# Moving one VectorE sum ahead of a scaled addition and a transposition in a graph layer and attention kernel

## The chip, the cores and the metric

The kernel runs on one core of a Trainium2 chip. The metric is device time in microseconds (us), the median of several executions. The engines are TensorE (PE in the profile, with its weight loads as PEld), VectorE (DVE), ScalarE (ACT), GpSimd (POOL) and SyncE (SP). In this kernel SP issues all DMAs of the main loop. Each engine works through its own list of instructions in order and waits on semaphores for the others.

## The reference

There are 64 batch elements of 256 nodes with 512 features, and one 256 x 256 graph. Two layers follow each other:

```python
# layer 0: graph layer, then residual and layer norm
mi, mj = x @ Wi.T, x @ Wj.T
a   = adj.astype(float);  deg = a.sum(axis=1)
out = deg[:, None] * (mi + b) + a @ mj
h   = layernorm(x + out)
# layer 1: attention over 8 heads of 64, masked by adj, then residual and layer norm
q, k, v = heads(h @ Wq.T + bq), heads(h @ Wk.T + bk), heads(h @ Wv.T + bv)
attn = softmax(where(adj == 0, -inf, q @ k.T / 8))
y    = layernorm(h + merge(attn @ v) @ Wo.T + bo)
```

All is float32. The change lies in layer 0, in the part that makes `mj`, and in the sum `x + deg * mi`.

## The kernel before

**Groups.** The elements are handled in 32 groups of two. A pass of the main loop (`for g in range(NG - 1)`, 31 passes, fully unrolled) does the attention of group g and, between its products, layer 0 of group g + 1. `b1` and `b2` are the first and the second element of a group. A row tile is 128 of the 256 nodes; `t` is 0 or 1.

**Products.** The dense products of layer 0 are done by blocks with seven products in place of eight. `l0_steps(b)` gives the steps of one element as a list of functions: `step1` to `step7` (each with one product of four matmuls on PE and what is done with its result), `neighbours` (the product with the graph), `take(1)` and `take(0)` (the residual sum and the statistics of the norm), and `give` and `send_h` for each row tile (the norm applied, and h sent to DRAM to be read back in another layout).

The steps around the change, in the names of the code:

- `step4` keeps `u2` (L542, DVE), `step5` copies a product into `mj[:, 1]` (L547, DVE).
- `step6` makes `u3` (L551, DVE). POOL adds it to `mj[:, 1]` (L552). `split(1)` then makes the high half `hi` on ACT (L524) and the low half `lo` = `mj` - `hi` on POOL (L525), since the graph product takes its operands in a shorter format and two halves keep the precision. At the end of the step `add_scaled(1, u3)` (L520, DVE) adds `deg * u3` to row tile 1 of `xh`, where the residual is gathered.
- `step7` makes `mj[:, 0]` from its product and `u2` (L561, DVE), and `split(0)` makes its two halves.
- `neighbours` multiplies `hi` and `lo` of both row tiles by the graph into `pa`, row tile 1 of `mj` first.
- `take(t)` adds `pa` to `xh` (L575, DVE) and computes the statistics (L453 to L459 on DVE, the power `rstd` on POOL, L461).

**Where they run.** `layer0(g)` cuts the steps of both elements into portions, and the main loop runs one portion after each pair of attention products. In the portion concerned stands also `turn_h(b1)`: a DVE transposition (L485) of the first element's h, which has come back from DRAM in the tile `hB`, into `hT`. The next portion starts after the last two value products of the pass and is written out by hand: first product of the output projection (`o[0]`), `neighbours`, `take(1)`, `take(0)`, first product of the query projection (`q[0]`), and so on. `multiply` (L844, POOL) scales the attention output, `divide` has the reciprocal of the denominators (L882, DVE) and the DMAs `spread` (L890), eight for each reciprocal. The first product of the output projection is added on POOL (L746, L747).

**What sets the order.** A scheduler orders the instructions of each engine by the order of the program and by times that it reckons for them. An instruction that goes through `in_order` keeps its place among the others of its engine that do; one that doesn't (`anywhere`) may be moved. All matmuls, the transpositions, and the operations of `take` and `give` are held in order; L561 and the scaled addition are not:

```python
def in_order(ins):
    tc.keep_in_program_order(ins)

def anywhere(ins):
    pass
```

The weight factors of layer 1 come from DRAM through a ring of 9 buffers (L442), the products of layer 0 and of the projections share three PSUM banks (tag "mm"), and `hi`, `lo`, `mj`, `hB` and `hT` have one buffer each. L740 (DVE) adds later products of the output projection to `xh` and frees their banks.

Of the kernel before, what the change touches and what calls it, by code (L numbers as in the profile page):

```python
# [12 lines left out]
ALU = mybir.AluOpType  # L13
# [211 lines left out]
def unshifted_path(ctx, tc, flag, x, adj, wiT, wjT, b0, wqT, bq, wkT, bk, wvT, bv, woT, bo, out):  # L225
# [16 lines left out]
    nc = tc.nc  # L242
# [26 lines left out]
    def bank(name):  # L269
        return ps_m.tile([P, 512], F32, tag="mm", name=name)  # L270

    def score_banks(name):
        return ps_s.tile([P, 2, 512], F32, tag="sc", name=name)
# [8 lines left out]
    def in_order(ins):  # L282

        tc.keep_in_program_order(ins)
# [4 lines left out]
    def matmul(*args, **kw):  # L289
        in_order(nc.tensor.matmul(*args, **kw))  # L290
# [5 lines left out]
    xh = {}  # L296
# [47 lines left out]
    deg = small.tile([P, NT], F32, tag="deg", name="deg")  # L344
# [51 lines left out]
    def blocks_of(w):  # L396
        return (w.rearrange("(h c p) (j o) -> p h c j o", h=2, p=P, j=2) if w is woT else
                w.rearrange("(p h c) (j o) -> p h c j o", h=2, p=P, j=2))

    sources = {}  # L400
    for name, w in (("wq", wqT), ("wk", wkT), ("wv", wvT), ("wo", woT)):
        src = blocks_of(w)
# [48 lines left out]
    def norm_stats(t, order=anywhere):  # L451
        st = small.tile([P, 6], F32, tag="st", name="st")
        order(nc.vector.bn_stats(st, t))  # L453
        mv = small.tile([P, 2], F32, tag="mv", name="mv")
        nc.vector.bn_aggr(mv, st)
        ve = small.tile([P, 1], F32, tag="ve", name="ve")
        nc.vector.tensor_scalar(ve, mv[:, 1:2], EPS, None, ALU.add)
        below = small.tile([P, 1], F32, tag="below", name="below")
        order(nc.vector.tensor_scalar(below, mv[:, 0:1], -1.0, None, ALU.mult))  # L459
        rstd = small.tile([P, 1], F32, tag="rstd", name="rstd")  # L460
        nc.gpsimd.tensor_tensor(rstd, ve, mhalf, ALU.pow)  # L461
        return below, rstd

    def norm_apply(t, below, rstd, order=anywhere):
        shift = small.tile([P, 1], F32, tag="shift", name="shift")
        order(nc.scalar.activation(shift, below, AF.Identity, scale=rstd))  # L466
        order(nc.scalar.activation(t, t, AF.Identity, bias=shift, scale=rstd))  # L467
# [31 lines left out]
            for step in left_steps(xS[b], in_order):  # L499
                step()  # L500

    def l0_steps(b):
        banks, k = {}, {}

        def product(name, left, n, first):
            if first:
                banks[name] = bank("po")
            for c in range(2):
                matmul(banks[name], left[:, c, :], w0[:, n, c, :], start=(first and c == 0),
                                 stop=(c == 1), skip_group_check=True)  # L510

        def raw(t, h):
            return xT[b][:, 2 * h:2 * h + 2, t * P:(t + 1) * P]

        def keeper(name):
            k[name] = p3.tile([P, D], F32, tag="lu", name=name)
            return k[name]

        def add_scaled(t, src):
            nc.vector.scalar_tensor_tensor(xh[b][:, t, :], src, deg[:, t:t + 1], xh[b][:, t, :],  # L520
                                           ALU.mult, ALU.add)

        def split(t):
            nc.scalar.copy(k["hi"][:, t, :], k["mj"][:, t, :])  # L524
            nc.gpsimd.tensor_tensor(k["lo"][:, t, :], k["mj"][:, t, :], k["hi"][:, t, :].bitcast(F32),  # L525
                                    ALU.subtract)

        def step1():
            product("x", raw(0, 0), B11, True)
            nc.scalar.copy(keeper("u1"), banks["x"])  # L530

        def step2():
            product("w", raw(1, 1), T4, True)
            add_scaled(1, banks["w"])

        def step3():
            product("x", raw(0, 1), B21, False)
            add_scaled(0, banks["x"])

        def step4():  # L540
            product("y", xS[b]["S2"], T2, True)
            nc.vector.tensor_add(keeper("u2"), banks["y"], k["u1"])  # L542

        def step5():
            product("z", xS[b]["S1"], T1, True)
            k["mj"] = p1.tile([P, NT, D], F32, tag="mj", name="mj")
            nc.vector.tensor_copy(k["mj"][:, 1, :], banks["z"])  # L547

        def step6():
            product("y", xS[b]["S3"], T3, False)  # L550
            nc.vector.tensor_add(keeper("u3"), banks["y"], k["u1"])  # L551
            nc.gpsimd.tensor_tensor(k["mj"][:, 1, :], k["mj"][:, 1, :], k["u3"], ALU.add)  # L552

            k["hi"] = p1.tile([P, NT, D], F32R, tag="hi", name="hi")
            k["lo"] = p1.tile([P, NT, D], F32R, tag="lo", name="lo")
            split(1)
            add_scaled(1, k["u3"])

        def step7():
            product("z", xS[b]["S4"], B22, False)  # L560
            nc.vector.tensor_add(k["mj"][:, 0, :], banks["z"], k["u2"])  # L561
            split(0)

        stats = {}

        def neighbours():
            k["pa"] = score_banks("pa")
            for i in (1, 0):
                for n, (j, part) in enumerate((j, part) for j in (1, 0) for part in ("hi", "lo")):
                    matmul(k["pa"][:, i, :], graph[:, j, i * P:(i + 1) * P], k[part][:, j, :],  # L570
                           start=(n == 0), stop=(n == 2 * NT - 1))

        def take(t):
            r = xh[b][:, t, :]
            in_order(nc.vector.tensor_add(r, k["pa"][:, t, :], r))  # L575
            stats[t] = norm_stats(r, in_order)

        def give(t):
            norm_apply(xh[b][:, t, :], *stats[t], in_order)


        return [step1, step2, step3, step4, step5, step6, step7, neighbours, lambda: take(1), lambda: take(0),
                lambda: give(1), lambda: send_h(b, 1), lambda: give(0), lambda: send_h(b, 0)]

# [10 lines left out]
    def send_h(b, t):  # L595
        i = b % NB
        if t == 1:
            h_cols[b] = dram.tile([D // P, N, P], F32, tag=f"h{i}", name="h_cols")
        nc.sync.dma_start(out=h_cols[b][:, t * P:(t + 1) * P, :].rearrange("q p n -> p q n"),
                          in_=xh[b][:, t, :].rearrange("p (q n) -> p q n", n=P))  # L600
        if t == 0:
            hB[b] = p1.tile([P, N // R, P], F32, tag="hB", name="hB")
            nc.sync.dma_start(out=hB[b].rearrange("p a n -> p (a n)"),
                              in_=h_cols[b].rearrange("q (r a) n -> (q r) (a n)", r=R))
# [63 lines left out]
    def second_late(steps):  # L668
        return [steps[0], steps[2], steps[1], *steps[3:]]
# [30 lines left out]
    def qk_steps(g, store, tag, bias, diff, early=False):  # L700

        def new_store():
            store[g] = p1.tile([P, NC, NB * N], F32, tag=tag, name=tag)

        def place(i, j):
            return store[g][:, 2 * j:2 * j + 2, i * N:(i + 1) * N]

        def biased(b):
            def evict(dst, ps):
                for m in range(2):  # L710
                    nc.scalar.activation(dst[:, m, :], ps[:, m, :], AF.Identity, bias=b[:, m:m + 1], scale=1.0)
            return evict

        def last(dst, ps, addend):
            for m in range(2):
                nc.vector.scalar_tensor_tensor(dst[:, m, :], ps[:, m, :], diff[:, m:m + 1],
                                               addend[:, m, :], ALU.add, ALU.add)

        return qkv_steps(g, True, new_store, place, biased(bias), biased(diff), last, early)
# [175 lines left out]
    def layer0(g):  # L895

        b1, b2 = NB * g, NB * g + 1

        def item(f, *args):
            return lambda: f(*args)  # L900

        p, q = l0_steps(b1), l0_steps(b2)
        return [p[:3] + [item(turn_x, b2)] + p[3:4],
                p[4:7] + [item(sum_x, b2), item(add_bias, b2)] + q[:1],
                p[7:10], p[10:] + q[1:3],
                q[3:6] + [item(turn_h, b1)] + q[6:7],
                q[7:], [item(turn_h, b2)]]

    def run(steps):
# [6 lines left out]
    def order_of(name):  # L916
        return [(name, n) for n in RIGHT]

    for g in range(-1, NG - 1):
        o, q, k, v = (order_of(name) for name in ("wo", "wq", "wk", "wv"))  # L920
# [18 lines left out]
    p, q = l0_steps(0), l0_steps(1)  # L939
# [19 lines left out]
    k = second_late(qk_steps(0, kT, "kT", bk_sb, bkd, True))  # L959
# [22 lines left out]
    for g in range(NG - 1):  # L982
# [20 lines left out]
        q = second_late(qk_steps(g + 1, qT, "qT", bq_sb, bqd))  # L1003
        k = second_late(qk_steps(g + 1, kT, "kT", bk_sb, bkd, True))
# [7 lines left out]
        k = with_output_bias(g + 1, k)[2:]  # L1012
# [101 lines left out]
```

## Time and profile before

| | |
|---|---|
| runs | 3117.25 us median of 3 (3113.67 to 3117.7) |
| profiled execution: span and the time listed for it | 3114.5 us |
| TensorE clock granted | 0.999 |
| PE, PEld busy | 3066.7 us (98%), 2125.4 us (68%) |
| DVE busy | 2200.1 us (71%) |
| POOL busy | 1505.3 us (48%) |
| ACT busy | 967.4 us (31%) |
| DMA engines busy | 48.4% in the main queue |

"Busy" is the time in which an engine executed instructions; its waits and the issue of DMAs are not in it. In the lines of a timeline the columns are the start, the duration (both us), the engine, the line of the code, the operation, what it writes and reads (`out<-in`), the shapes, how many were merged into the line, and in brackets the idle time before it with what ended it. In the list of waits a line names who waited for whom, with the total, how often, and the longest. All matmuls are recorded by one helper (L290), so that they are told apart by the tiles they write.

### The profile page before, as it was taken

To read this page: it belongs to the slowest core of one execution; us is meant where nothing else is said; L and a number is where in the kernel's file an instruction comes from. 1 tells how busy PE (TensorE), PEld (TensorE's weight loads), DVE (VectorE), ACT (ScalarE), POOL (GpSimd) and SP (SyncE) were. 2 spreads that over 40 slices of the span, in tenths; PEclk is the share of its full clock that TensorE was granted. 3 is DMA by queue.
4 is the path that set the end of the run, shared out by engine and by line. 5 is a ranking of instruction groups with operands and counts; after the bars stand their busy time and mean duration, and the time that the engine had idled before them with its cause. 6 is when DMAs were issued, how large, how long until landed. Compare 5 with 4: busy or idle time off the path is not lost. (4 is left out here: it accounts for less than half of the span.)

```text
span 3114.5 us, 42683 instructions
## 1 busy us (share of the span) xinstructions
PE 3066.7 (98%) x14598; PEld 2125.4 (68%) x14598; DVE 2200.1 (71%) x3298; ACT 967.4 (31%) x1861; POOL 1505.3 (48%) x1255
## 2 busy tenths in 40 slices
PE   8999999999999999999999999999999999999998
PEld 4667766677766777666776667776677766677665
DVE  6776677766777767777667776677766777767775
ACT  2322333323333323332233332333332333323332
POOL 2544445544545445454454554454543545445453
PEclk9999999999999999999999999999999999999999
DMA  7355544455444555345553445544455444555333
GB/s 253 116 151 156 166 122 131 133 155 165 143 123 125 157 165 152 117 129 151 156 166 119 129 135 158 164 142 124 124 159 164 144 123 125 158 158 158 119 106 103
DMA packets 410395, 447.28 MB, mean 144 GB/s; under 512 B 40896, under 2 KB 300224, under 8 KB 409792
## 3 DMA queue, kind: packets, MB, share of 16 engines
q1 hardware_dynamic: 410176, 444.50, 48.4%
q8 instruction: 120, 1.97, 0.3%
q14 instruction: 99, 0.81, 0.1%
HBM read 340.79 MB, written 70.25 MB: 132 GB/s over the span
## 5 line engine op out<-in xcount | busy, mean ns | idle before, releaser
L461 POOL TENSOR_TENSOR rstd<-ve,mhalf 128x1 f32<-128x1 f32 x256 | 140.4, 552 | 715.8 <-DVE below L459 715.8
L812 POOL TENSOR_TENSOR pk<-pe 128x512 f32<-128x512 f32 x256 | 322.5, 1276 | 327.6 <-ACT pe L809 327.5
L290 PE MATMUL po<-w,xS 128*128 128x512 f32 x1024 | 462.4, 599 | 0.4 <-DVE xS L478 0.4
L290 PE MATMUL st<-hS,factor 128*128 128x256 f32 x2048 | 453.5, 380 | 5.1 <-DVE xh L740 3.8
L290 PEld LDWEIGHTS st<-hS,factor 128*128 128x128 f32 x2048 | 388.9, 190 | 60.1 <-DVE xh L740 6.4
L809 ACT ACTIVATE pe<-pe 128x1024 f32<-128x1024 f32 x256 | 270.9, 1058 | 379.0 <-DVE pe L805 379.0
L290 PE MATMUL po<-w,xT 128*128 128x512 f32 x768 | 354.5, 605 | 13.1 <-DVE xT L485 11.1
L290 PE MATMUL st<-hT,factor 128*128 128x256 f32 x1536 | 352.6, 380 | 0.7 <-ACT hT L622 0.7
L290 PEld LDWEIGHTS po<-w,xS 128*128 128x128 f32 x1024 | 190.1, 191 | 235.9 <-issue 206.4
L805 DVE TENSOR_TENSOR pe<-ps,maskT 128x1024 f32<-128x1024 f32 x256 | 298.1, 1195 | 35.3 <-PE ps L290 35.3
L290 PEld LDWEIGHTS st<-hT,factor 128*128 128x128 f32 x1536 | 292.2, 190 | 41.7 <-ACT hT L622 0.9
L882 DVE RECIPROCAL rden<-den 128x256 f32<-128x256 f32 x127 | 223.1, 1757 | 92.2 <-PE den L290 89.0
L290 PEld LDWEIGHTS po<-w,xT 128*128 128x128 f32 x768 | 144.7, 192 | 181.2 <-issue 163.3
L290 PE MATMUL ps<-qT,kT 64*128 64x256 f32 x2048 | 265.0, 393 | 0.0
L290 PE MATMUL pav<-pe,v_sb 128*64 128x256 f32 x2048 | 250.2, 386 | 1.9 <-ACT pe L809 1.8
L883 POOL TENSOR_TENSOR rtot<-rtot,rden 128x256 f32<-128x256 f32 x127 | 92.3, 727 | 329.7 <-DVE rden L882 329.7
L740 DVE TENSOR_TENSOR xh<-st,xh 128x512 f32<-128x512 f32 x186 | 144.6, 777 | 136.4 <-PE st L290 136.4
L290 PEld LDWEIGHTS pav<-pe,v_sb 128*64 128x64 f32 x2048 | 135.3, 136 | 154.0 <-issue 95.4
L290 PEld LDWEIGHTS ps<-qT,kT 64*128 64x128 f32 x2048 | 184.7, 187 | 77.8 <-issue 51.3
L290 PE MATMUL st<-factor,hS 128*128 128x256 f32 x1024 | 234.8, 383 | 0.0
L525 POOL TENSOR_TENSOR lo<-mj,hi 128x512 fp32r<-128x512 f32 x128 | 175.2, 1378 | 107.3 <-ACT hi L524 107.3
L290 PE MATMUL st<-factor,oS 128*128 128x256 f32 x992 | 224.3, 380 | 0.0
(115 smaller groups left out, 4679.5 us busy)
## 6 DMA issues: line engine op xcount, KB each, us to landing
xB<-in_x_dram SPq DMA_DIRECT2D x256, 128.0 KB, 3.8
xh<-in_x_dram SPq DMA_DIRECT2D x64, 512.0 KB, 4.2
factor<-wq SPq DMA_DIRECT2D x128, 256.0 KB, 4.3
factor<-wk SPq DMA_DIRECT2D x128, 256.0 KB, 3.0
factor<-wv SPq DMA_DIRECT2D x128, 256.0 KB, 2.7
spread<-rden SPq DMA_DIRECT2D x1016, 32.0 KB, 1.9
factor<-wo SPq DMA_DIRECT2D x124, 256.0 KB, 3.2
h_cols<-xh SPq DMA_DIRECT2D x124, 256.0 KB, 2.4
```

Source lines behind the costliest of these rows:

```text
L290: in_order(nc.tensor.matmul(*args, **kw))
L461: nc.gpsimd.tensor_tensor(rstd, ve, mhalf, ALU.pow)
L525: nc.gpsimd.tensor_tensor(k["lo"][:, t, :], k["mj"][:, t, :], k["hi"][:, t, :].bitcast(F32), ALU.subtract)
L740: nc.vector.tensor_add(dst, src, dst)
L805: nc.vector.tensor_add(pe.rearrange("p j t q -> p j (t q)"), ps.rearrange("p j t q -> p j (t q)"), maskT.rearrange("p t q -> p (t q)").uns ...
L809: in_order(nc.scalar.activation(flat, flat, AF.Exp, scale=QSCALE, accum_out=etot[:, NB * g + i, pr:pr + 1]))
L812: nc.gpsimd.tensor_tensor(pk, pe[:, :, 0, :], pe[:, :, 1, :], ALU.add)
L882: nc.vector.reciprocal(rden, den)
L883: nc.gpsimd.tensor_tensor(rtot, rtot, rden, ALU.add)
```

## The change

`l0_steps` gets an argument `late`, which only the second element's steps in the main loop set. With it, `add_scaled(1, u3)` is left out of `step6` and issued in `take(1)`, in order, right before `pa` is added to the same rows; the sum of `step7` is held in order; and `layer0` runs `step7` whole before the transposition of the first element's h rather than after it.

```diff
-    def l0_steps(b):
+    def l0_steps(b, late=False):
         banks, k = {}, {}
+        order = in_order if late else anywhere
...
         def add_scaled(t, src):
-            nc.vector.scalar_tensor_tensor(xh[b][:, t, :], src, deg[:, t:t + 1], xh[b][:, t, :],
-                                           ALU.mult, ALU.add)
+            return nc.vector.scalar_tensor_tensor(xh[b][:, t, :], src, deg[:, t:t + 1], xh[b][:, t, :],
+                                                  ALU.mult, ALU.add)
...
             split(1)
-            add_scaled(1, k["u3"])
+            if not late:
+                add_scaled(1, k["u3"])
 
         def step7():
             product("z", xS[b]["S4"], B22, False)
-            nc.vector.tensor_add(k["mj"][:, 0, :], banks["z"], k["u2"])
+            order(nc.vector.tensor_add(k["mj"][:, 0, :], banks["z"], k["u2"]))
             split(0)
...
         def take(t):
             r = xh[b][:, t, :]
+            if late and t == 1:
+                in_order(add_scaled(1, k["u3"]))
             in_order(nc.vector.tensor_add(r, k["pa"][:, t, :], r))
...
-        p, q = l0_steps(b1), l0_steps(b2)
+        p, q = l0_steps(b1), l0_steps(b2, True)
...
-                q[3:6] + [item(turn_h, b1)] + q[6:7],
+                q[3:7] + [item(turn_h, b1)],
```

## The prediction

> **What bounds the kernel.** I read the page first (busy shares), then the list of waits for PE alone, then the timeline of one loop pass engine by engine. The page:
>
> ```profile
> PE 3066.7 (98%) x14598; PEld 2125.4 (68%) x14598; DVE 2200.1 (71%) x3298; ACT 967.4 (31%) x1861; POOL 1505.3 (48%) x1255
> ```
>
> PE is occupied from end to end; no other engine comes near. So only what shortens or removes a PE wait can pay, and only what creates one can cost. The list of waits, PE's own (columns: total us, times, longest):
>
> ```profile
> PE pa L290 <- POOL lo L525: 15.9, 31, 0.5
> PE po L290 <- DVE xT L485: 11.1, 2, 8.3
> PE st L290 <- DVE xh L740: 3.8, 5, 1.2
> ```
>
> The first wait happens 31 times, once per pass of the main loop: the neighbour product `pa` waits for the low half `lo`, which POOL makes. The second lies in the prologue, out of the change's reach. The third is rare; I return to it. Now the pass that starts its first-element transposition at 1000.78 us. Timeline of DVE (start us, duration us):
>
> ```profile
> 999.00 1.86 DVE L520 SCALAR_TENSOR_TENSOR xh<-u,deg,xh 128x512 f32<-128x512 f32 x1
> 1000.78 2.14 DVE L485 STREAM_TRANSPOSE hT<-hB 128x1024 f32<-128x1024 f32 x1
> 1002.83 0.64 DVE L561 TENSOR_TENSOR mj<-po,u 128x512 f32<-128x512 f32 x1
> 1003.40 1.74 DVE L882 RECIPROCAL rden<-den 128x256 f32<-128x256 f32 x1
> 1006.99 0.69 DVE L575 TENSOR_TENSOR xh<-pa,xh 128x512 f32<-128x512 f32 x1 [1.86 <-PE pa L290]
> ```
>
> The sum of row tile 0 (L561) has no idle time before it: it is not waiting for its product but standing behind 1.86 us of scaled addition and 2.14 us of transposition. POOL in the same pass, after its L552 of 999.04 to 1000.31 (the sum of row tile 1):
>
> ```profile
> 1001.04 1.29 POOL L525 TENSOR_TENSOR lo<-mj,hi 128x512 fp32r<-128x512 f32 x1 [0.73 <-ACT hi L524]
> 1004.20 1.29 POOL L525 TENSOR_TENSOR lo<-mj,hi 128x512 fp32r<-128x512 f32 x1 [1.86 <-ACT hi L524]
> 1005.44 1.29 POOL L844 TENSOR_TENSOR aoT<-aoT,spread 128x512 f32<-128x512 f32 x1
> 1006.68 0.73 POOL L883 TENSOR_TENSOR rtot<-rtot,rden 128x256 f32<-128x256 f32 x1
> 1007.37 1.27 POOL L746 TENSOR_TENSOR xh<-xh,u 128x512 f32<-128x512 f32 x1
> 1008.60 2.36 POOL L747 TENSOR_TENSOR xh<-xh,u 128x1024 f32<-128x1024 f32 x1
> 1010.91 1.06 POOL L461 TENSOR_TENSOR rstd<-ve,mhalf 128x1 f32<-128x1 f32 x2
> ```
>
> The second L525 (row tile 0) idles 1.86 us, then runs to 1005.49, and PE continues at once:
>
> ```profile
> 1003.97 0.58 PE L290 MATMUL pa<-hi,graph 128*128 128x512 f32 x1
> ...
> 1004.62 0.39 PE L290 MATMUL pa<-hi,graph 128*128 128x512 f32 x1
> 1005.54 0.50 PE L290 MATMUL pa<-lo,graph 128*128 128x512 f32 x1 [0.52 <-POOL lo L525]
> ...
> 1006.79 0.38 PE L290 MATMUL st<-hT,factor 128*128 128x256 f32 x1
> ```
>
> The same eight matmuls in the prologue, where nothing is late:
>
> ```profile
> 53.74 0.58 PE L290 MATMUL pa<-hi,graph 128*128 128x512 f32 x1
> ...
> 55.80 1.02 PE L290 MATMUL st<-hT,factor 128*128 128x256 f32 x4
> ```
>
> **What the Trainium skill says.** "Perfetto Trace Analysis", section "Identifying the Most-Contended Engine", warns that matmul busy time is no measure of headroom, because matmuls are pipelined. The trace agrees: the wait is booked as 0.52 us, but the group takes 1006.79 - 1003.97 = 2.82 us against 55.80 - 53.74 = 2.06. I therefore price the stall by start times, not by idle time. "SBUF — State Buffer", section "Who interferes with whom", says that a VectorE instruction with two SBUF inputs and a GpSimd instruction that reads SBUF exclude each other, the second to start waiting in full, while one SBUF input does not contend. The trace agrees: the scaled addition from `u3` (two SBUF inputs) took 1.86 us beside L552, ending 0.55 after L552 let go at 1000.31, while the same operation with a PSUM input takes 0.74 (mean of that group), beside POOL or not.
>
> **The change, part by part.** In each of 31 passes it leaves every instruction and every DMA as it was; three DVE instructions change places. No DMA moves in the program's order, but the transfers that wait for these results shift with them.
>
> (a) *The sum goes ahead of addition and transposition.* It needs its product. Products of this element arrive 1.72 us apart (L547 at 996.55 and L551 at 998.27 both waited for PE), so this one arrives at 998.27 + 1.72 = 999.99. DVE is free since L551 ended at 998.96. The sum runs 999.99 to 1000.68, with one SBUF input, so L552 beside it doesn't matter. Being held in order now, it makes the transposition behind it wait for PE as well; that is the new wait. The transposition then runs 1000.68 to 1002.82, 0.1 us earlier than before: the wait costs nothing because the addition used to stand in its place.
>
> (b) *What follows the sum.* ACT finishes the high half of row tile 1 at 1000.96, then does that of tile 0 to about 1001.6. POOL does L525 of tile 1 to 1002.33 as before and of tile 0 to 1003.62. PE wants it 0.23 us after 1004.62, at 1004.85. Slack 1.2 us: the stall is gone. Worth 2.82 - 2.06 = 0.76 us per pass; 31 x 0.76 = **23.6 us**.
>
> (c) *The reciprocal* follows the transposition at 1002.82 instead of 1003.40 and ends at 1004.56. The eight `spread` DMAs that wait for it on SP start 0.6 us earlier, and so does what SP has behind them (weight factors, the sends of h).
>
> (d) *The scaled addition* now stands before L575. I take it behind the reciprocal, at 1004.56. POOL has moved up: L844 runs 1003.62 to 1004.91 (its last `spread` was issued by 999.75 and such DMAs land in 1.9 us by the page). So the addition waits for the port until 1004.91 and ends 0.55 later, at 1005.46. Bounds: 0.74 us unblocked, 1.86 us as seen, so 1005.3 to 1006.4. L575 can start only when `pa` is complete, 1006.99 - 0.76 = 1006.23. DVE idled 1.86 us there; that idle time is the cover. If it were gone, L575, the statistics, the powers on POOL and the sends of h would be late; even the upper bound makes L575 only 0.2 us late.
>
> (e) *Does something late eat the gain?* The statistics' powers (L461) wait on POOL behind L883, L746 and L747. From 1005.46 these take 0.73 + 1.27 + 2.36, so L461 starts at 1009.82 instead of 1010.91: 1.09 us earlier, while PE gains only 0.76. The chain from there (shift and scaling on ACT, two sends to DRAM, the load of hB, the second element's transposition, its sums, then L740 freeing a bank for PE) keeps its durations, so it gains 0.33 us on PE. That shortens the third wait of PE, 5 x 0.33 = 1.7 us of its 3.8.
>
> Sum: -23.6 - 1.7 = -25.3 us. The profiled execution's span is 3114.5 us and that is the time listed for it; the median of the runs lies 2.75 us above. The saving is in the loop, so it applies to both: 3117.25 - 25.3 = **3092 us** (span about 3089).
>
> **Rivals.** (1) *Given back at the second element's h.* DVE waits for hB at only 6 transpositions, and PE for the following L740 at only 5 passes, yet the margin is small. If the chain of (e) doesn't move, for instance because transfers take longer when issued closer together, PE gains 0.76 and then loses what exceeds the margin; in the pass above the wait was already 0.4. A give-back of 0.3 to 0.5 us per pass leaves 31 x 0.26 to 0.46 = 8 to 14 us: 3103 to 3109. Against it: POOL's earlier powers.
>
> (2) *The addition is put ahead of the reciprocal*, since only the addition is held in order. It would start at 1002.82, be blocked by L525 to 1003.62, end at 1004.17; the reciprocal ends at 1005.91, 0.8 us later than before, and so do the `spread` DMAs. L461 starts at about 1010.3, 0.6 us earlier, against 0.76 on PE: 5 waits grow by 0.16, about 1 us. L844's second product slips too; PE uses it over 2 us later (1013.22 to 1015.42). 3117 - 23.6 + 1 to 4 = 3095 to 3098.
>
> (3) *Slower: the addition loses the port again and again.* POOL's work from L844 to L747 has no gaps. If DVE gets the port only when POOL idles, the addition ends around 1009.8 and L575 starts there, 2.8 us late. The powers then come at about 1011.6, 0.7 us later than before, and PE stalls before L740 by that, plus its 0.76 gain, less some 0.5 of margin (0.2 at the bank and 0.3 at the load of hB): net +0.2 us a pass, 3117 + 7 = 3124. It decides from an L575 after about 1009.3. Against it: the addition of 999.00 finished 0.55 us after one POOL instruction, but there POOL then paused; no row shows this instruction between back-to-back ones.
>
> (4) *The change doesn't do what it says*: if `lo` of tile 0 stays behind L844 or its cast is placed late, the stall stays: 3115 to 3119. Both orders follow the program's today, which speaks against it.
>
> **How the numbers follow.** The forecast 0.80; rival 1 0.06; rival 2 0.06; rival 3 0.05; rival 4 0.03. The likeliest case spans 3087 (all of the 3.8 gone, and a little more) to 3098. To take in most of rival 2 and the better part of rival 1, the range reaches 3106. About 0.2% (6.2 us) is what a measurement of this kernel can tell from no change. Faster: the forecast, rival 2 and nearly all of rival 1, 0.91. Same: most of rival 4 and a little of rivals 1 and 3, 0.04. Slower: 0.05.
>
> **What would show it.** Right: no row "PE pa <- POOL lo" among PE's waits; the second L525 directly behind the first, without idle time; L561 ahead of L485 with about 1.0 us of idle time for PE; `pa` groups of 2.06 us from first start to the next product; L461 over 0.7 us earlier against the transposition; the L740 wait at most as large as before. Wrong: a "PE st <- DVE L740" row of many passes (rival 1), the reciprocal behind the scaled addition (rival 2), a scaled addition of over 3 us (rival 3), or an unchanged `pa` row (rival 4).

## The result and the profile after

The changed kernel takes 3088.62 us in the median of 5 runs (3086.21 to 3090.58), the kernel before 3116.09 us in the median of 5 (the table above has the first three of them). The ratio is 0.9918 with an interval from 0.9906 to 0.993: 27.5 us less, where 25.3 was forecast (3092 us, range 3086 to 3106). A second measurement on another occasion gave 0.9919 (0.9906 to 0.9933). The profiled execution has a span of 3084.3 us against 3114.5 us, and a time of 3086.33 us.

Where a changed kernel is spoken of, the line numbers are those of its file, in which the same lines stand lower: by one from L520 to L552 (so that L521 is the scaled addition, L525 and L526 make `hi` and `lo`, L552 makes `u3`), by two at the sum of row tile 0 (L563 for L561), and by four from L575 on (L579, L744, L750, L751, L848, L886 and L887 for L575, L740, L746, L747, L844, L882 and L883).

The page's line of busy times, after:

```profile
PE 3055.9 (99%) x14598; PEld 2122.5 (69%) x14598; DVE 2176.4 (71%) x3298; ACT 974.7 (32%) x1861; POOL 1519.8 (49%) x1255
```

PE issues the same 14598 matmuls in 30.2 us less span. PE's own waits, after (total us, times, longest):

```profile
PE po L290 <- DVE xT L485: 10.9, 2, 8.1
...
PE st L290 <- DVE xh L744: 0.2, 1, 0.2
```

The row of `pa` and POOL's `lo` is gone altogether, the one in the prologue stands, and the wait for the line that was L740 fell from 3.8 us in 5 passes to 0.2 us in one. The same pass as before in the timeline of DVE (start us, duration us):

```profile
989.78 0.69 DVE L552 TENSOR_TENSOR u<-po,u 128x512 f32<-128x512 f32 x1 [1.02 <-PE po L290]
991.50 0.69 DVE L563 TENSOR_TENSOR mj<-po,u 128x512 f32<-128x512 f32 x1 [1.02 <-PE po L290]
992.10 2.18 DVE L485 STREAM_TRANSPOSE hT<-hB 128x1024 f32<-128x1024 f32 x1
994.18 1.75 DVE L886 RECIPROCAL rden<-den 128x256 f32<-128x256 f32 x1
995.83 1.05 DVE L521 SCALAR_TENSOR_TENSOR xh<-u,deg,xh 128x512 f32<-128x512 f32 x1
997.73 0.69 DVE L579 TENSOR_TENSOR xh<-pa,xh 128x512 f32<-128x512 f32 x1 [0.86 <-PE pa L290]
```

The sum (L563) now waits 1.02 us for its product, 1.72 us after L552, exactly in the rhythm of the products, and the transposition begins at its end. The addition sits between reciprocal and the sum with `pa`, which still has 0.86 us to spare. POOL in that pass:

```profile
992.55 2.54 POOL L526 TENSOR_TENSOR lo<-mj,hi 128x512 fp32r<-128x512 f32 x2 [0.73 <-ACT hi L525]
995.02 1.30 POOL L848 TENSOR_TENSOR aoT<-aoT,spread 128x512 f32<-128x512 f32 x1
996.26 1.21 POOL L887 TENSOR_TENSOR rtot<-rtot,rden 128x256 f32<-128x256 f32 x1
997.42 1.27 POOL L750 TENSOR_TENSOR xh<-xh,u 128x512 f32<-128x512 f32 x1
998.65 2.36 POOL L751 TENSOR_TENSOR xh<-xh,u 128x1024 f32<-128x1024 f32 x1
1000.97 1.07 POOL L461 TENSOR_TENSOR rstd<-ve,mhalf 128x1 f32<-128x1 f32 x2
```

Both low halves run in one piece ("x2", 2.54 us). L887 took 1.21 us where it took 0.73 before: it began while the addition on DVE still had the port, and ended 0.59 us after it. And PE:

```profile
995.48 0.58 PE L290 MATMUL pa<-hi,graph 128*128 128x512 f32 x1
...
996.37 0.39 PE L290 MATMUL pa<-lo,graph 128*128 128x512 f32 x1
...
997.53 1.24 PE L290 MATMUL st<-hT,factor 128*128 128x256 f32 x5
```

From the first matmul of `pa` to the next product it is 997.53 - 995.48 = 2.05 us, the 2.06 of the prologue, where it was 2.82.

Laying the starts of all matmuls of the two traces side by side, pass for pass, gives the account: in the median pass the kernel before falls behind by 0.67 us at the fourth matmul of `pa` (the wait) and by another 0.10 at the fifth, and by nothing anywhere else. That is 0.78 us, over 31 passes 24.1 us. In the mean of the passes it is 0.92 us; the further 0.14 us, over 31 passes 4.3 us, is in the few passes in which L740 held PE up. The rest of the 30.2 us lies outside the loop: the first transposition of an h comes 1.8 us earlier in this execution (136.6 us after the start, not 138.4). In the profiles of all kernels of this document that start lay between 134.8 and 139.5 us, so I put it down to no part of the change.

### The profile page after: what moved, and what is told of

Same layout as the page of the kernel before. It is cut to its first block, busy times and chain, and to the rows that moved or that the text cites. A ratio compares the mean times of both kernels' runs of the same rounds, so it can differ in the third digit from the quotient of the medians.

```text
span 3084.3 us, 42714 instructions
## 1 busy us (share of the span) xinstructions
PE 3055.9 (99%) x14598; PEld 2122.5 (69%) x14598; DVE 2176.4 (71%) x3298; ACT 974.7 (32%) x1861; POOL 1519.8 (49%) x1255
## 5 line engine op out<-in xcount | busy, mean ns | idle before, releaser
L813 ACT ACTIVATE pe<-pe 128x1024 f32<-128x1024 f32 x256 | 270.8, 1058 | 379.0 <-DVE pe L809 379.0
L886 DVE RECIPROCAL rden<-den 128x256 f32<-128x256 f32 x127 | 222.6, 1753 | 92.1 <-PE den L290 89.0
L887 POOL TENSOR_TENSOR rtot<-rtot,rden 128x256 f32<-128x256 f32 x127 | 106.9, 841 | 329.4 <-DVE rden L886 329.4
L744 DVE TENSOR_TENSOR xh<-st,xh 128x512 f32<-128x512 f32 x186 | 144.5, 777 | 131.7 <-PE st L290 131.7
L290 PEld LDWEIGHTS st<-factor,hS 128*128 128x128 f32 x1024 | 191.9, 190 | 35.4 <-issue 10.6
```

The lines of the kernel that those rows point to most:

```text
L744: nc.vector.tensor_add(dst, src, dst)
L813: in_order(nc.scalar.activation(flat, flat, AF.Exp, scale=QSCALE, accum_out=etot[:, NB * g + i, pr:pr + 1]))
L886: nc.vector.reciprocal(rden, den)
L887: nc.gpsimd.tensor_tensor(rtot, rtot, rden, ALU.add)
```

## Experiments

**Is either move enough?** Four kernels on one chip; the first is the changed kernel as the yardstick. On the two other chips used further down the changed kernel was not timed again. The kernel before was, and its medians (3112.99, 3113.23 and 3112.93 us) lie within 0.3 us of each other, so that times are compared across the chips.

> The changed kernel once more, as the yardstick of the other three on this chip: 3086 to 3091 us as measured before, 27 us under the kernel before. Both theories say the same here.

Measured: 3087.75 us against 3112.99 us, ratio 0.9919 (0.9906 to 0.9933).

The sum alone goes ahead:

```diff
-            if not late:
+            if True:
                 add_scaled(1, k["u3"])
...
-            if late and t == 1:
-                in_order(add_scaled(1, k["u3"]))
```

> Only the sum of row tile 0 goes ahead of the transposition; the scaled addition stays where it was, in front of both. Theory A (the gain is the wait of PE for lo, and the new order has more room than it needs): counted from the pass at 1000 us of the kernel before, the addition ends at 1000.86, the sum at 1001.55, the cast at 1002.2, and lo of tile 0 still runs right behind lo of tile 1, 1002.33 to 1003.62, before PE needs it at 1004.85. The wait is gone, pa groups take 2.1 us, and the time is that of the full change: 3086 to 3092. Theory B (both moves are needed to clear the wait): a part of the wait stays, 0.2 to 0.5 us per pass, and the time is 3095 to 3108.

Measured: 3093.64 us (3087.73 to 3093.8), ratio 0.9937 (0.9923 to 0.995). POOL in a pass of its trace:

```profile
994.43 2.55 POOL L526 TENSOR_TENSOR lo<-mj,hi 128x512 fp32r<-128x512 f32 x2 [0.73 <-ACT hi L525]
```

The two low halves run in one piece and no wait of PE for `lo` is left. Theory A holds for the wait; but the median time lay 6 us above the changed kernel, just beyond the range I gave. The trace is of the fastest execution, 3087.73 us, and can't show that gap; the other four took 3092.6 to 3093.8 us. The gap got a test of its own below.

The addition alone moves:

```diff
-        order = in_order if late else anywhere
+        order = anywhere
...
-                q[3:7] + [item(turn_h, b1)],
+                q[3:6] + [item(turn_h, b1)] + q[6:7],
```

> Only the scaled addition moves to the front of the sum with pa; the sum of row tile 0 stays behind the transposition. Theory A: the transposition starts at about 999.0 and ends at 1001.1, the sum at 1001.8, the cast at 1002.45, lo of tile 0 at about 1003.7, again before 1004.85: no wait, 3086 to 3092. Theory B: the 2.14 us of the transposition in front of the sum keep a part of the wait, 3095 to 3108.

Measured: 3089.45 us (3086.44 to 3089.86), ratio 0.9924 (0.991 to 0.9938). DVE in a pass of its trace:

```profile
990.43 2.12 DVE L485 STREAM_TRANSPOSE hT<-hB 128x1024 f32<-128x1024 f32 x1
992.44 0.65 DVE L563 TENSOR_TENSOR mj<-po,u 128x512 f32<-128x512 f32 x1
994.01 1.76 DVE L886 RECIPROCAL rden<-den 128x256 f32<-128x256 f32 x1 [0.91 <-PE den L290]
```

and POOL:

```profile
992.61 2.50 POOL L526 TENSOR_TENSOR lo<-mj,hi 128x512 fp32r<-128x512 f32 x2 [0.73 <-ACT hi L525]
```

The transposition starts where the addition used to, and the sum ends at 993.1, early enough for both low halves to run in one piece. Theory B falls: each move alone clears the wait. To put the sum ahead of both is more than the wait needed. Moving the addition alone can't be told apart from the full change.

**Has the new order room?**

```diff
-            order(nc.vector.tensor_add(k["mj"][:, 0, :], banks["z"], k["u2"]))
+            for _ in range(2 if late else 1): order(nc.vector.tensor_add(k["mj"][:, 0, :], banks["z"], k["u2"]))
```

> The changed kernel with the sum of row tile 0 of the second element computed twice, 0.69 us more on VectorE per pass at the place of the change; the result is the same. Theory A (PE is the bound and the sum has slack): lo of tile 0 stays behind lo of tile 1 and does not move; transposition, reciprocal and addition come 0.69 us later, inside the idle time before the sum with pa (0.87 us in the changed kernel). No more than 0.3 us per pass, so 3087 to 3098, most likely 3090. Rival (VectorE has become the bound in this stretch): 31 x 0.69 = 21 us more, about 3110.

Measured: 3090.41 us, ratio 0.993 (0.9917 to 0.9944): 2.7 us over the changed kernel, not 21, and with an interval that overlaps that of the changed kernel. The addition and the sum with `pa` in a pass of its trace:

```profile
997.20 0.62 DVE L521 SCALAR_TENSOR_TENSOR xh<-u,deg,xh 128x512 f32<-128x512 f32 x1
998.39 0.69 DVE L579 TENSOR_TENSOR xh<-pa,xh 128x512 f32<-128x512 f32 x1 [0.57 <-PE pa L290]
```

Of 0.86 us of idle time 0.57 are left, although DVE had some 0.7 us more to do: the addition now takes 0.62 us in place of 1.05, since it comes late enough not to wait for L848. With four sums in place of two:

> The changed kernel with the second element's sum of row tile 0 computed four times (same result), 2.07 us more on VectorE per pass. Theory A: lo of tile 0 ends at about the moment PE wants it, so that pa hardly waits (0 to 0.2 us), but transposition, reciprocal, addition, the sum with pa and all behind them come 1.2 to 2 us later, past the room of 0.9 us at the load of hB; PE waits for that DVE line (L744 here) 0.5 to 1 us in most passes: 15 to 40 us over the changed kernel, 3103 to 3128. Rival (the order has room for 2 us of VectorE work): within 5 us of the changed kernel.

Measured: 3107.9 us, ratio 0.9984 (0.9976 to 0.9992), some 20 us over the changed kernel. The range was right, the place not. The waits of PE's weight loads in this trace:

```profile
PEld st L290 <- ACT u L715: 12.1, 31, 0.4
...
PEld pa L290 <- POOL lo L526: 11.0, 31, 0.4
...
PEld st L290 <- DVE xh L744: 5.6, 10, 1.3
```

The `lo` wait is back a little, as said (start by start it costs 0.18 us a pass). But L744, which I had expected in most passes, is the least of the three; a line of ACT that I had not had in mind costs most (L715, 0.25 us a pass).

**What was the wait of before worth?** The kernel before, with the sum doubled behind the transposition:

```diff
-    def l0_steps(b):
+    def l0_steps(b, twice=False):
...
-            nc.vector.tensor_add(k["mj"][:, 0, :], banks["z"], k["u2"])
+            for _ in range(2 if twice else 1): nc.vector.tensor_add(k["mj"][:, 0, :], banks["z"], k["u2"])
...
-        p, q = l0_steps(b1), l0_steps(b2)
+        p, q = l0_steps(b1), l0_steps(b2, True)
```

> The kernel before with the sum of row tile 0 of the second element computed twice in the loop (same result), 0.66 us more on VectorE in front of the cast. Theory A (in the order before, lo of tile 0 sits on PE's path without any slack): PE's wait for lo grows from 0.5 to about 1.2 us in each of 31 passes, the pa groups from 2.85 to 3.5 us, and the time by 31 x 0.66 = 20 us over the kernel before of this chip, to about 3133 if that is 3113. Rival (the booked wait is a matter of how matmuls are recorded, with little time behind it): within 5 us of the kernel before.

Measured: 3136.85 us against 3113.23 us, ratio 1.0077 (1.0061 to 1.0092), 23.6 us more. Waits of PE and of its weight loads (line numbers of the kernel before):

```profile
PE pa L290 <- POOL lo L525: 26.3, 31, 0.9
...
PEld pa L290 <- ACT hi L524: 16.9, 31, 0.6
```

The time was real, and without slack: 0.66 us of DVE work cost 0.71 us in each `pa` group (3.54 us in place of 2.82, mean of 31), 22 us in all. PE's booked wait for `lo` grew only from 15.9 to 26.3 us. Of the 0.71 us, start by start, 0.44 came at the fourth matmul and 0.27 at the third, which now had to wait for `hi` of row tile 0; that second wait stands only in the list of the weight loads, where the kernel before has no such row. A change in PE's own list is not the change in time.

**Why did the wait for L740 shrink?** The chain that I had named runs from the powers on POOL over ACT and two DMAs to the load of hB. Powers that come later again, here because each is computed three times, should bring the wait back:

```diff
-    def norm_stats(t, order=anywhere):
+    def norm_stats(t, order=anywhere, times=1):
...
-        nc.gpsimd.tensor_tensor(rstd, ve, mhalf, ALU.pow)
+        for _ in range(times): nc.gpsimd.tensor_tensor(rstd, ve, mhalf, ALU.pow)
...
-            stats[t] = norm_stats(r, in_order)
+            stats[t] = norm_stats(r, in_order, 3 if late else 1)
```

> The changed kernel with the second element's powers (rstd on GpSimd) computed three times each in the loop (same result): the first comes 1.1 us later, the second 2.1, about what the change had gained for them. Theory C (the third wait, for L740 behind the load of hB, shrank because this chain came earlier than PE did): the sends come some 0.9 us later, the load of hB loses its room of 0.9 us in the median pass, and PE waits again for that DVE line in ten or more passes, 3 to 12 us in all: 3091 to 3100. Rival D (that wait depends only on chance in the transfers): unchanged, 3086 to 3090, with the wait in 0 to 2 passes.

Measured: 3103.3 us, ratio 0.9971 (0.9959 to 0.9982): 15 us over the changed kernel, more than either theory. The waits of PE and its weight loads:

```profile
PEld st L290 <- ACT u L715: 16.5, 31, 0.5
...
PE st L290 <- DVE xh L744: 2.1, 3, 1.1
```

L744 came back in 3 passes, not in ten or more: theory C explains 2 us of it. The other 12 are at one product: start by start, PE loses 0.40 us per pass at the second key product. That product adds to the bank of the first, which ACT must have read (`u`, L715); and ACT stands behind shift and scaling of row tile 1, which wait for the first power. Two kernels tell the paths apart. Only the power of row tile 1 tripled (that of row tile 0 stands behind it on POOL and comes later too):

```diff
-            stats[t] = norm_stats(r, in_order, 3 if late else 1)
+            stats[t] = norm_stats(r, in_order, 3 if late and t == 1 else 1)
```

> The kernel with the powers computed three times lost most of its 15 us at another place than the third wait: in its trace PE loses 0.40 us per pass at the second key product, whose bank ACT has to read first (u<-st, L715), and ACT stands behind the shift and scaling of row tile 1. Here only the power of row tile 1 is computed three times (same result). Theory G (the loss is this line of ACT): the same 0.40 us per pass at the same product, 31 x 0.40 = 12 us over the changed kernel, 3098 to 3104. Theory C (the loss comes from the load of hB and the wait for L744): a good part of it goes, 3090 to 3096.

Measured: 3104.25 us, ratio 0.9974 (0.9963 to 0.9984), a quarter of a microsecond above the range of theory G and far from that of theory C. Its PE loses 0.39 us a pass at that product, and the waits of its weight loads have the same row:

```profile
PEld st L290 <- ACT u L715: 16.2, 31, 0.5
```

Timeline of ACT, first of this kernel, then of the changed one:

```profile
1008.55 0.81 ACT L467 ACTIVATE xh<-xh,shift,rstd 128x512 f32<-128x512 f32 x1
1009.27 0.82 ACT L715 ACTIVATE u<-st,bk 128x256 f32<-128x256 f32 x2
```

```profile
1001.88 0.81 ACT L467 ACTIVATE xh<-xh,shift,rstd 128x512 f32<-128x512 f32 x1
1002.91 0.84 ACT L715 ACTIVATE u<-st,bk 128x256 f32<-128x256 f32 x2 [0.21 <-PE st L290]
```

In the changed kernel ACT waits 0.21 us for PE there; with the later power ACT has no idle time left, and PE waits for ACT. The same with `t == 0`:

> Only the power of row tile 0 is computed three times (same result); it ends about 1.1 us later, at the moment when ACT turns to the shift of row tile 0 anyway. Theory G: the copy for the second key product stands ahead of it on ACT and is not held up, so no loss there; the time is that of the changed kernel within 3 us, 3086 to 3091. Theory C: the send of row tile 0 is the one that ends the chain to hB, so that a later power costs as much as in the kernel with both tripled, 3095 to 3103.

Measured: 3088.97 us, ratio 0.9922 (0.9908 to 0.9935), the time of the changed kernel. So theory G holds: it is the power of row tile 1 that PE feels, through ACT; that of row tile 0 could come over 1 us later at no cost. ACT's 0.21 us is not the whole room, though. With the power of row tile 1 tripled, ACT began the shift 1.26 us later (median pass, counted from the last matmul of `pa`), and PE's start at the second key product slipped by only 0.29 us, before the further 0.10 at the next matmul. That leaves, as an estimate, 1.26 - 0.29 = 0.97 us of room. The kernel with four sums gives the same, a shift 1.12 us later and 0.15 us lost. In the kernel before, the shift came 0.67 us later than in the changed one by this count, inside that room, and PE lost nothing there.

**What does the addition's move add?** The kernel with only the sum moved, again:

> The kernel with only the sum moved, once more, since its times went from 3087.7 to 3093.8. Theory E (leaving the addition in front delays the reciprocal by 0.8 us and the spread transfers by 0.4, these bunch with the weight factors and the send of h, whose write then lands 0.7 us later, so that hB has 0.4 us of room in place of 0.9 and some executions lose it): again 3 to 6 us over the changed kernel, ratio to the kernel before 0.993 to 0.995. Rival F (chance): ratio 0.991 to 0.9925 as for the changed kernel.

Measured: 3094.02 us (3091.6 to 3096.41), ratio 0.9939 (0.9926 to 0.9953); in both measurements some 6 us over the changed kernel, as much as theory E says. Waits of PE in its trace, here of an execution of 3094.37 us:

```profile
PE st L290 <- DVE xh L744: 4.3, 9, 1.2
```

Start by start, PE loses 6.8 us more than in the changed kernel at the two matmuls where it waits for L744, and hardly anything elsewhere in the loop. SP's waits (L607 is the load of hB), changed kernel first, then this one:

```profile
SPq L607 <- DMA h_cols<-xh: 161.8, 62, 4.4
```

```profile
SPq L607 <- DMA h_cols<-xh: 186.8, 62, 4.8
```

The load of hB waits 25 us longer in all for the write of h. The send is issued at the same moment in both (17.0 us after L548), but the write lands 5.5 us after its issue in the median pass instead of 4.6. The reciprocal starts 6.87 us after L548 where it was 6.10, and the first `spread` transfer is issued at 8.66 us where it was 8.24; so the transfers in front of the send stand closer together. Then hB is there on average as DVE turns to it (room in the median pass 0.04 us, 0.88 in the changed kernel; 0.37 in the fast execution of the first measurement, where PE waited once for L744). That the room is lost and that the write is slower is measured; that this crowding slows it is inferred from the times of issue and wasn't tried by itself.

## Why the prediction was right

- **The wait for `lo` goes, for 0.76 us a pass.** Right in mechanism and size: 0.78 by the starts of the matmuls, and no row is left. Pricing by starts and not by the booked 0.52 us was the step that mattered; the booked sum would have given 15.9 us. The kernel with the doubled sum in the old order confirms the price from the other side.
- **(a), (b): the sum at 1.72 us after L551, both low halves back to back.** Right to the hundredth for the sum. The room of 1.2 us was real (the low halves end at 995.09, the fourth matmul of `pa` starts at 996.37), and it was more than the wait needed: either move alone would do.
- **(c): the `spread` transfers 0.6 us earlier.** The reciprocal ended 0.74 us earlier counted from L551, but SP issued the first of them only 0.40 us earlier.
- **(d), (e): the addition blocked by L844, then blocking L883.** Right: 1.05 us measured against 0.90, and L887 stretched to 1.21. Rival 3 falls by this row: between GpSimd instructions without a gap DVE got the port at the first boundary, in each of the 31 passes (1.09 us at most). So what the Trainium skill says in "SBUF — State Buffer", section "Who interferes with whom", was borne out in the new place too.
- **(e): the chain to hB gains on PE.** Right in direction, mis-sized: the powers came 1.44 us earlier counted from L551 (1.09 predicted), because the addition ended 0.09 us earlier than in my sum, L887 ended 0.59 us after it where I had added 0.73, and each of the next three instructions starts 0.04 to 0.05 us before the end of the one in front of it, where I had put them end to end. The third wait fell by 3.6 us where I took 1.7; by size that is most of the 2.2 us by which the forecast was short, but these 2.2 us lie inside the interval of the measurement (22 to 29 us), so that how close the total came is in part luck. The size of that wait is not proportional to the room: room in the median pass of 0.37 us (before) went with 5 passes that waited, 0.30 (both powers tripled) with 3, 0.04 (only the sum moved, second measurement) with 9, 0.88 (changed) with 1.
- **Not seen:** the second key product behind ACT. It didn't hurt, since the powers came early; but with both powers late it took back 12 us and the load of hB only 2. Rival 3, and rival 1 as far as it means late powers, were priced by the wrong path. The other half of rival 1, transfers that take longer and eat the room at hB, is what the kernel with only the sum moved shows on a small scale: 6 us.
- **Rivals 2 and 4** did not happen: the reciprocal stayed ahead of the addition, and the casts kept their places.

None of the variants beats the changed kernel. In its loop PE's matmuls have 0.2 us of booked waits left, those for L744; the 1.8 us for L813 (two waits) lie behind the loop, in the attention of the last group.

## What to carry to other kernels

When the busiest engine waits at the same place in every pass, look at what stands in front of the producer in its own queue: here 4 us of work that nobody needed yet stood ahead of 0.7 us that PE was waiting for, with no dependency between them. Moving either piece of that work out of the way was enough. Price such a stall by comparing starts with a group that didn't wait, not by the booked idle time. Then follow every later chain to its next reader on each engine's queue, also the ones that look idle: the first place where PE felt late powers was not the place where it already waited.

## What I had not expected of the hardware

A wait inside a stream of matmuls cost PE another 0.10 us at the matmul after the one that waited, on top of the wait itself. It did so each time: at `pa` in the kernel before, with the doubled sum in the old order and with four sums; at the second key product with late powers (0.104 us); and after the rare waits for L740 and L744 (0.104 us too), whether the wait was 0.1 or 1.4 us long. What makes it so is open. And a wait of about 0.3 us in each of 31 passes, at the second key product, shows nowhere among PE's matmul waits; only the list for its weight loads has it.
